# The third hop's result transposed back on 64-row halves of TensorE, with layer 1's other terms in the batches' own order

## The chip, the cores and the metric

The kernel runs on one core of a Trainium2 chip. The metric is the device time of one execution in microseconds, given as the median of several runs. The profile is of one execution, and has its own time.

## The reference, cut to what matters

Two graph layers act on x of 8 batches, 2048 nodes and 64 features. The adjacency `adj` is 2048 x 2048 with random places; in each row all non-zero entries are equal.

```python
# layer 0: weights of its own for each node, from a 16-wide embedding
w = einsum('nd,dkio->nkio', embedding, weight)      # 3 terms k
As = [I, A, 2*(A @ A) - I]
out = einsum('bnki,nkio->bno', einsum('knm,bmc->bnkc', As, x), w) + b
x = layernorm(x + out)
# layer 1: the same two supports, both adj, five terms
x_cat = [x0, A x0, 2 A A x0 - x0, A x0, 2 A A x0 - x0]
out = concat(x_cat) @ weight + bias
x = layernorm(x + out)
```

So there are four products with A ("hops"), two for each layer. For layer 1 the kernel folds the five weights into three, V0, V1 and V2, and computes h V0 + A (h V1 + A (h V2)), where h is layer 0's output. The third hop is A times (h V2), the fourth A times the bracket.

## The kernel before, in words

The 2048 nodes are 16 tiles of 128 rows. A tile of features is 128 nodes by 512 columns (8 batches x 64 features). The values of A are replaced by zeros and ones and a factor for each row (`rcol`), and each feature matrix is split into a high and a low part in a rounded fp32 type, so that two matmuls make up one product.

Stages, in order of time:

1. The first hop (`hop_x`, `add_block`, line 231) and the second hop. The second and the third are done by `seven_products`: A is cut into 2 x 2 quarters, the features too, and seven products of quarters take the place of eight. Line 558 is their matmul. Their result comes out transposed: features on the partitions, nodes along the columns.
2. Layer 0's node-wise mixing (`mix0`, lines 340 to 370): for each tile the operands are transposed (`transpose`, line 274, already on 64-row halves of the array, one half for each of two batches), multiplied with the weights (line 361) and added up on VectorE (line 367). Then comes the layer norm, then `project`.
3. `project` (lines 372 to 390) multiplies a tile of h by the three folded weights (line 380). ScalarE copies the terms h V2 and h V1 to `z[0]` and `z[1]` (line 387), VectorE adds a bias to h V0 and writes it to `z[2]` (line 388). The last tile's `project` runs inside the third hop, after 64 of its matmuls.
4. The third hop (`third`, lines 679 to 683). Its seven products accumulate in two sets of PSUM banks, `sums3[0]` and `sums3[1]`, in turn. `put` (line 577) adds each product to the quarters of the transposed result `zT` in SBUF. When a quarter is finished, `quarter_back` (line 669) queues work in `todo`: `back` (lines 656 to 663) transposes its blocks on TensorE into PSUM banks that are free at that time, and `add_back` (lines 665 to 667) adds them on VectorE, scaled by `rcol`, to `z[1]`. Three of the four quarters go that way, 16 transposes of 128 x 128 each (line 662). The fourth is done inside the fourth hop, at its steps 1 and 3 (lines 791 to 795), 8 transposes each.
5. The fourth hop (`hop_g` and `hop_tile`, lines 767 to 844; line 231), layer 1's norm, and the stores.

`run` (line 242) writes out the order by hand: each step consists of parts with a lead (operands are made up to six steps ahead), and after each step two entries of `todo` are taken. From the last tile of layer 0 to the end of the fourth hop's first part, the order on each engine is kept as written (`in_order`, `ordered`).

The order of batches is what the change turns on. Among four batches of a group g, x has batch number 4g + 2i + j. `mix0` writes it to place 4g + 2j + i (the pattern `(j i)`), and h keeps that mixed order. `project` reads h in halves (its index j is a half of TensorE's rows, i a block of columns) and writes all three terms with the pattern `(i j)`, so they stay in the mixed order up to the output, and the host permutes the output at the end. `back` handles blocks of 128 columns, each with two neighbouring places, whose features lie on the lower and the upper 64 partitions of `zT`.

Of the kernel before, what the change touches and what calls it, by code (L numbers as in the profile page):

```python
# [17 lines left out]
P = 128  # L18
B, N, C = 8, 2048, 64
NT = N // P  # L20
# [17 lines left out]
def pattern(  # L38
# [22 lines left out]
    nc = tc.nc  # L61
# [20 lines left out]
    def bank(name):  # L82

        return psum.tile([P, 2, 512], F32, tag="ps", name=name)
# [7 lines left out]
    z = [z0, [z1[:, t, :] for t in range(NT)], [z2[:, t, :] for t in range(NT)]]  # L92

    def bc(s, t):
        return z[s][t].rearrange("p (b c) -> p b c", c=C)
# [10 lines left out]
    ident = keep.tile([P, P], F32, tag="ident", name="ident")  # L106
# [15 lines left out]
    def ordered(ins):  # L122
        if in_order:
            tc.keep_in_program_order(ins)
# [247 lines left out]
    def project(t, hT, pus=None):  # L372


        for g in range(2):
            pm = bank("pu") if pus is None else pus[g]
            for i in range(2):
                for j in range(2):
                    q = slice(j * C, (j + 1) * C)
                    nc.tensor.matmul(  # L380
                        pm[:, j, i * 3 * C : (i + 1) * 3 * C], lhsT=hT[q, 2 * g + i, :], rhs=v[q],
                        start=True, stop=True,
                    )
            got = pm[:, :, : 6 * C].rearrange("p j (i k c) -> p j i k c", i=2, k=3)
            to = [bc(k, t)[:, 4 * g : 4 * g + 4, :].rearrange("p (i j) c -> p j i c", j=2) for k in range(3)]
            for k in range(2):
                ordered(nc.scalar.copy(to[k], got[:, :, :, 2 - k, :]))
            ordered(nc.vector.tensor_tensor(
                to[2], got[:, :, :, 0, :], bias1.unsqueeze(1).unsqueeze(1).to_broadcast([P, 2, 2, C]), ALU.add,
            ))  # L390
# [4 lines left out]
    BC = B * C // 2  # L395
# [242 lines left out]
    zT, tpool = {}, ExitStack()  # L638
# [6 lines left out]
    def last_projected():  # L645
        project(NT - 1, last_h["T"], (sums3[1][1], sums3[1][0]))
        layer0.close()
        t_pool = pool(tpool, "fzT", 1, reuse_waits="tile")
        for a in range(2):
            for c in range(2):  # L650
                zT[a, c] = t_pool.tile([P, 4, B * C], F32, tag=f"zT{a}{c}", name="zT")
# [3 lines left out]

    def back(ts, pairs, b):

        to = [pairs[n // 4][:, n // 2 % 2, n % 2 * BC : (n % 2 + 1) * BC] for n in range(len(ts))]
        for t, a in zip(ts, to):
            for i in range(2):  # L660
                block = slice((2 * b + i) * P, (2 * b + i + 1) * P)
                nc.tensor.transpose(a[:, i * P : (i + 1) * P], zT[t // 8, t // 4 % 2][:, t % 4, block], ident)  # L662
        return to

    def add_back(t, a, b):
        to = z[1][t][:, b * BC : (b + 1) * BC]
        ordered(nc.vector.scalar_tensor_tensor(to, a, rcol[:, t : t + 1], to, ALU.mult, ALU.add))

    def quarter_back(a, b, which):
        ts, got = range(8 * a, 8 * a + 8), []  # L670

        def two(n):
            for m in (n, n + 1):
                add_back(ts[m], got[m], b)

        work_here = [nothing, nothing, lambda: got.extend(back(ts, sums3[which], b)), nothing]
        return work_here + [lambda n=n: two(n) for n in range(0, 8, 2)]
# [20 lines left out]
    for t in range(NT):  # L698
# [11 lines left out]
        if t == NT - 1:  # L710

            in_order.append(True)
            at = {(1, 0): [between], (1, 1): [lambda: project(t - 1, done["hT"])]}
# [10 lines left out]
        if t > 0:  # L724
            project(t - 1, done["hT"])
# [41 lines left out]
    def hop_g(k):  # L767
# [12 lines left out]
        def use(got):  # L780
            s, hl, end = got["s"], hls[k], k == NT - 1
            if k == 0:
                pairs = [*sums3[1], sums3[0][0]]
                accs[:] = [p[:, i] for p in pairs for i in range(2)]
            add_block(accs[:4], s, hl, k == 0, end)
            waiting.append((s[:, 4 * P :], hl, k == 0, end))
            if k > 0:

                while waiting:
                    add_block(accs[4:], *waiting.pop(0))  # L790
            if k in (1, 3):

                ts = range(8, 12) if k == 1 else range(12, NT)
                for t, a in zip(ts, back(ts, [sums3[0][1]], 0)):
                    add_back(t, a, 0)
            if end:
                for t, a in enumerate(accs):
                    evict(z[2][t], t, a, t % 2)
                bank("skip")
# [53 lines left out]
def general(  # L853
# [10 lines left out]
    nc = tc.nc  # L864
# [11 lines left out]
    z = [zpool.tile([P, 2, B, C], F32, tag=f"z{t}", name=f"z{t}") for t in range(NT)]  # L876


    ident = const.tile([P, P], F32, tag="ident", name="ident")
# [52 lines left out]
    def next_order(o):  # L932

        return o[NT - SLOTS :] + o[: NT - SLOTS]
# [23 lines left out]
    def transpose(src, tag):  # L958

        tt = work.tile([P, B // 2, P], F32, tag=tag, name=tag)  # L960
        pt = ps_tp.tile([P, B // 2, P], F32, tag="tp", name="pt")
        for j in range(B // 2):
            nc.tensor.transpose(pt[:, j, :], src[:, 2 * j : 2 * j + 2, :], ident)
        nc.scalar.copy(tt, pt)
        return tt
# [66 lines left out]
    def project(t, h, u):  # L1032

        hT = transpose(h, "hT")
        for g in range(2):
            pm = ps_mix.tile([P, 2, 512], F32, tag="mix", name="pu")
            for i in range(2):
                for j in range(2):
                    q = slice(j * C, (j + 1) * C)
                    nc.tensor.matmul(  # L1040
                        pm[:, j, i * 3 * C : (i + 1) * 3 * C], lhsT=hT[q, 2 * g + i, :], rhs=v[q],
                        start=True, stop=True,
                    )
            got = pm[:, :, : 6 * C].rearrange("p j (i k c) -> p j i k c", i=2, k=3)
            bs = slice(4 * g, 4 * g + 4)
            for k in range(2):
                nc.scalar.copy(u[t][:, k, bs, :].rearrange("p (i j) c -> p j i c", j=2), got[:, :, :, 2 - k, :])
            nc.vector.tensor_tensor(
                z[t][:, 0, bs, :].rearrange("p (i j) c -> p j i c", j=2), got[:, :, :, 0, :],
                bias1.unsqueeze(1).unsqueeze(1).to_broadcast([P, 2, 2, C]), ALU.add,  # L1050
            )

# [14 lines left out]
    u = [upool.tile([P, 2, B, C], F32, tag=f"u{t}", name=f"u{t}") for t in range(NT)]  # L1067
    order = list(range(NT))
# [6 lines left out]
    order = next_order(order)  # L1075
# [3 lines left out]
    for i, t in enumerate(order):  # L1079
        if behind is not None:  # L1080
            bt, x2 = behind
            tt = [transpose(z[bt][:, 0], "t0"), transpose(z[bt][:, 1], "t1"), transpose(x2, "t2")]
        ph = hop(t, lambda k: z[k][:, 1], ks)
        x2 = work.tile([P, B, C], F32, tag="x2", name="x2")
        nc.vector.scalar_tensor_tensor(x2, ph, 2.0, z[t][:, 0], ALU.mult, ALU.subtract)
        prefetch(order, i, 1)
        if mixed is not None:
            project(*mixed, u)
        if behind is not None:
            mixed = bt, mix0(bt, tt)  # L1090
        behind = (t, x2)
    bt, x2 = behind
    tt = [transpose(z[bt][:, 0], "t0"), transpose(z[bt][:, 1], "t1"), transpose(x2, "t2")]
    project(*mixed, u)
    project(bt, mix0(bt, tt), u)
    ks = order
    order = next_order(order)
# [7 lines left out]
    order = next_order(order)  # L1105
# [66 lines left out]
```

## Time and profile before

| | |
|---|---|
| median of 3 runs | 828.28 us (827.91 to 828.90) |
| the profiled execution's own time | 828.66 us |
| its span, first to last instruction | 826.8 us |
| mean granted TensorE clock | 0.997 |
| TensorE busy | 812.6 us |
| VectorE busy | 594.7 us |
| ScalarE busy | 275.3 us |
| third hop, from its first matmul to the fourth hop's first | 587.0 to 698.7 us |
| fourth hop, to the start of the last chain of norm and store | 698.7 to 809.5 us |
| transposes of `back`, line 662 | 64 of 128 x 128, from 656.8 us on |

A line such as "L662 PE MATMUL accT<-ident,zT" names the line of the kernel, the engine, the operation, and the tiles written and read. PE is TensorE's matmul, PEld its weight load, DVE is VectorE, ACT ScalarE, POOL GpSimd, SP the engine that issues most loads. Matmuls overlap and their ends are modelled, so a group's cost shows in the starts of its matmuls and not in their durations.

### The profile page before, as it was taken

To read this page: it belongs to the slowest core of one execution; us is meant where nothing else is said; L and a number is where in the kernel's file an instruction comes from. 1 tells how busy PE (TensorE), PEld (TensorE's weight loads), DVE (VectorE), ACT (ScalarE), POOL (GpSimd) and SP (SyncE) were. 2 spreads that over 40 slices of the span, in tenths; PEclk is the share of its full clock that TensorE was granted. 3 is DMA by queue.
4 is the path that set the end of the run, shared out by engine and by line. 5 is a ranking of instruction groups with operands and counts; after the bars stand their busy time and mean duration, and the time that the engine had idled before them with its cause. 6 is when DMAs were issued, how large, how long until landed. Compare 5 with 4: busy or idle time off the path is not lost.

```text
span 826.8 us, 14470 instructions
## 1 busy us (share of the span) xinstructions
PE 812.6 (98%) x5614; PEld 725.2 (88%) x5614; DVE 594.7 (72%) x1303; ACT 275.3 (33%) x496; POOL 111.9 (14%) x121
## 2 busy tenths in 40 slices
PE   9999999999999999999999999999999999999995
PEld 6888888888788999999999999999878888888884
DVE  6878658763467888888888888888867546758762
ACT  5436445877401111111111101111287664203110
POOL 0000000000641111111110111111100000003341
PEclk9999999999999999999999999999999999999998
DMA  9997885544200000000000001130154435565631
GB/s 329 376 386 244 287 315 174 155 143 148 69 3 12 15 13 15 14 14 14 14 14 14 30 13 38 39 103 27 43 150 152 141 128 150 167 181 165 212 120 42
DMA packets 70940, 96.54 MB, mean 117 GB/s; under 512 B 4432, under 2 KB 45648, under 8 KB 70736
## 3 DMA queue, kind: packets, MB, share of 16 engines
q1 hardware_dynamic: 61616, 78.49, 29.5%
q10 hardware_dynamic: 6944, 8.66, 3.0%
q0 software_dynamic: 2304, 8.39, 2.8%
q8 instruction: 46, 0.75, 0.4%
q14 instruction: 30, 0.25, 0.1%
HBM read 78.75 MB, written 16.78 MB: 116 GB/s over the span
## 4 chain that ended last, share of the span: by engine, by line
PE 92%; issue 3%; DVE 3%; POOL 1%; ACT 1%; DVEq 0%; POOLq 0%; ACTq 0%
PE pm L361 36%; PE accT L558 24%; PE acc L231 14%; PE a L231 8%; PE accT L231 5%; PE pu L380 2%; DVE acc L367 2%; POOL z L609 1%; PE pt L274 1%; PE accT L662 1%; PE first L135 1%; POOL xc L322 0%; POOL got L337 0%; ACT sq L310 0%; DVE s L200 0%
## 5 line engine op out<-in xcount | busy, mean ns | idle before, releaser
L367 DVE SCALAR_TENSOR_TENSOR acc<-pm,pack_sb,acc 128x256 f32<-128x256 f32 x512 | 246.3, 483 | 41.6 <-PE pm L361 20.5
L558 PE MATMUL accT<-s,hl 128*128 128x512 f32 x896 | 205.6, 390 | 1.9 <-DVE s L200 1.4
L558 PEld LDWEIGHTS accT<-s,hl 128*128 128x128 f32 x896 | 167.6, 188 | 37.7 <-issue 1.8
L361 PE MATMUL pm<-w,xt 64*128 64x256 f32 x1024 | 160.9, 378 | 1.1 <-DVE acc L367 1.1
L361 PE MATMUL pm<-w,t 64*128 64x256 f32 x1024 | 160.0, 376 | 0.2 <-ACT t L276 0.2
L361 PE MATMUL pm<-w,z 64*128 64x256 f32 x1024 | 159.9, 376 | 0.0
L231 PE MATMUL acc<-hl,s 128*128 128x512 f32 x512 | 117.1, 390 | 0.0
L546 ACT CAST s<-raw 128x1024 fp32r<-128x1024 bf16 x96 | 101.0, 1052 | 40.2 <-ACT hl L211 32.2
L231 PEld LDWEIGHTS acc<-hl,s 128*128 128x128 f32 x512 | 95.8, 188 | 21.1 <-DVE hl L215 0.7
L361 PEld LDWEIGHTS pm<-w,t 64*128 64x128 f32 x1024 | 110.7, 187 | 1.9 <-ACT t L276 0.6
L361 PEld LDWEIGHTS pm<-w,z 64*128 64x128 f32 x1024 | 110.8, 187 | 1.4
L361 PEld LDWEIGHTS pm<-w,xt 64*128 64x128 f32 x1024 | 108.4, 187 | 2.5 <-issue 1.2
L276 ACT COPY hT<-pt 128x512 f32<-128x512 f32 x15 | 8.8, 587 | 197.4 <-PE pt L274 197.4
L231 PE MATMUL a<-hl,s 128*128 128x512 f32 x320 | 73.0, 389 | 0.0
L231 PEld LDWEIGHTS a<-hl,s 128*128 128x128 f32 x320 | 60.0, 188 | 12.5
L211 ACT CAST hl<-z 128x256 fp32r<-128x256 f32 (+1 forms) x96 | 47.1, 510 | 67.6 <-PE acc L231 36.4
L215 DVE TENSOR_TENSOR hl<-z,hl 128x512 fp32r<-128x512 f32 (+1 forms) x96 | 52.5, 552 | 21.2 <-ACT hl L211 18.4
L322 POOL TENSOR_TENSOR xc<-acc,s 128x512 f32<-128x512 f32 x16 | 16.7, 1043 | 279.5 <-DVE s L320 265.4
L200 DVE TENSOR_SCALAR s<-raw 128x1024 fp32r<-128x1024 f32 x47 | 33.2, 706 | 16.5 <-PE acc L231 10.9
L231 PE MATMUL accT<-hl,s 128*128 128x512 f32 x192 | 44.2, 390 | 0.0
L231 PEld LDWEIGHTS accT<-hl,s 128*128 128x128 f32 x192 | 35.9, 188 | 7.4
L347 POOL TENSOR_TENSOR acc<-z,ebias 128x256 f32<-128x256 f32 x32 | 22.7, 731 | 90.5 <-DVE hl L215 87.2
(105 smaller groups left out, 603.3 us busy)
## 6 DMA issues: line engine op xcount, KB each, us to landing
raw<-in_adj SPq DMA_DIRECT2D x67, 512.0 KB, 4.7
raw<-sums_of SPq DMA_DIRECT2D x64, 256.0 KB, 2.8
sums_of<-z POOLq DMA_DIRECT2D x16, 512.0 KB, 6.3
raw<-quarters SPq DMA_DIRECT2D x32, 256.0 KB, 2.6
raw<-in_adj SPq DMA_DIRECT2D x16, 384.0 KB, 3.5
quarters<-seen ACTq DMA_DIRECT2D x16, 256.0 KB, 6.2
xt<-in_xT SPq DMA_DIRECT2D x16, 256.0 KB, 2.6
out<-got ACTq DMA_DIRECT2D x16, 256.0 KB, 3.9
```

The source lines that it names most:

```text
L200: ordered(nc.vector.tensor_scalar(s, raw, 0.0, None, ALU.not_equal))
L211: ordered(nc.scalar.copy(to[0], src))
L215: ordered(nc.vector.tensor_tensor(to[1], src, to[0], ALU.subtract))
L231: nc.tensor.matmul(accs[i], lhsT=s[:, i * P : (i + 1) * P], rhs=hl[h], start=(first and h == 0), stop=(last and h == 1),)
L276: ordered(nc.scalar.copy(tt.rearrange("p j (h n) -> p h j n", h=2), pt[:, :, : B // 2 * C].rearrange("p h (j n) -> p h j n", n=C)))
L322: ordered(nc.gpsimd.tensor_tensor(xc, src, wide(s), ALU.subtract))
L347: nc.gpsimd.tensor_tensor(part.rearrange("p (j i) c -> p j i c", j=2), bc(0, t)[:, 4 * g : 4 * g + 4, :].rearrange("p (i j) c -> p j i c", ...
L361: nc.tensor.matmul(pm[:, j, i], lhsT=tt[k][q, 2 * g + i, :], rhs=w[k][q, ds, :], start=(k == 0), stop=(k == 2),)
L367: ordered(nc.vector.scalar_tensor_tensor(part, pm[:, :, :, d, :].rearrange("p j i c -> p (j i) c"), emb_sb[:, t, dd : dd + 1], part, ALU.m ...
L380: nc.tensor.matmul(pm[:, j, i * 3 * C : (i + 1) * 3 * C], lhsT=hT[q, 2 * g + i, :], rhs=v[q], start=True, stop=True,)
L546: ordered(nc.scalar.copy(s, got["raw"]))
L558: nc.tensor.matmul(acc[i][:, c], lhsT=hl[h][:, i * P : (i + 1) * P], rhs=S[:, c * 512 : (c + 1) * 512], start=(kk == 0 and h == 0), stop=( ...
```

## The change

`back` no longer transposes a 128 x 128 block in one instruction. It takes the lower and the upper 64 partitions of `zT` apart, with one transpose for each on its half of the array's rows (index j), 64 columns wide; each half's results go to a PSUM bank of its own. So there are 128 transposes in place of 64. A tile's result then lies in two banks, 128 columns in each, and its halves are ordered `(j i)`: the batches' own order. `add_back` reads this two-bank layout and adds it to `z[1]`. For the terms to fit together, `project` writes `z[1]` and `z[2]` in the pattern `(j i)` as well; `z[0]`, the operand of the third hop, stays in `(i j)`. The output is then in the batches' own order, and the host's permutation becomes a plain one. The fallback `general`, which runs only if a flag is set, gets the same change of order in its own `project`.

```diff
@@ project
-            to = [bc(k, t)[:, 4 * g : 4 * g + 4, :].rearrange("p (i j) c -> p j i c", j=2) for k in range(3)]
+            order = ["p (i j) c -> p j i c", "p (j i) c -> p j i c", "p (j i) c -> p j i c"]
+            to = [bc(k, t)[:, 4 * g : 4 * g + 4, :].rearrange(order[k], j=2) for k in range(3)]
@@ back
-        to = [pairs[n // 4][:, n // 2 % 2, n % 2 * BC : (n % 2 + 1) * BC] for n in range(len(ts))]
+        to = [pairs[n // 4][:, :, n % 4 * P : (n % 4 + 1) * P] for n in range(len(ts))]
         for t, a in zip(ts, to):
             for i in range(2):
                 block = slice((2 * b + i) * P, (2 * b + i + 1) * P)
-                nc.tensor.transpose(a[:, i * P : (i + 1) * P], zT[t // 8, t // 4 % 2][:, t % 4, block], ident)
+                for j in range(2):
+                    q = slice(j * C, (j + 1) * C)
+                    nc.tensor.transpose(
+                        a[:, j, i * C : (i + 1) * C], zT[t // 8, t // 4 % 2][q, t % 4, block], ident[q, q]
+                    )
@@ add_back
-        to = z[1][t][:, b * BC : (b + 1) * BC]
+        to = z[1][t][:, b * BC : (b + 1) * BC].rearrange("p (j n) -> p j n", j=2)
@@ kernel, on the host
-    got = got.reshape(NT, P, 2, 2, 2, C).transpose(2, 4, 3, 0, 1, 5)
-    return lay(got.reshape(B, N, C))
+    return lay(got.transpose(2, 0, 1, 3).reshape(B, N, C))
```

More of the change, by code (lines that the diff above doesn't have):

```diff
@@ L1046, in project @@
             for k in range(2):
-                nc.scalar.copy(u[t][:, k, bs, :].rearrange("p (i j) c -> p j i c", j=2), got[:, :, :, 2 - k, :])
+                nc.scalar.copy(u[t][:, k, bs, :].rearrange("p (j i) c -> p j i c", j=2), got[:, :, :, 2 - k, :])
             nc.vector.tensor_tensor(
-                z[t][:, 0, bs, :].rearrange("p (i j) c -> p j i c", j=2), got[:, :, :, 0, :],
+                z[t][:, 0, bs, :].rearrange("p (j i) c -> p j i c", j=2), got[:, :, :, 0, :],
                 bias1.unsqueeze(1).unsqueeze(1).to_broadcast([P, 2, 2, C]), ALU.add,
```

## The prediction

> **What bounds the kernel now.** I read the page first (busy shares, then the chain that ended last), then the chain in order of time around the change, then the rows of the transposes themselves, and last the starts of single matmuls.
>
> ```profile
> PE 812.6 (98%) x5614; PEld 725.2 (88%) x5614; DVE 594.7 (72%) x1303; ACT 275.3 (33%) x496; POOL 111.9 (14%) x121
> ...
> PE 92%; issue 3%; DVE 3%; POOL 1%; ACT 1%; DVEq 0%; POOLq 0%; ACTq 0%
> ```
>
> TensorE is busy for 98% of the span and makes 92% of the chain. So a change is worth what it takes from TensorE's own row of work, unless it is made in one of the few places where TensorE waits. The chain in order of time shows whether the third hop has such places:
>
> ```profile
> 606.15 51.09 PE accT L558 x224
> 657.24 1.75 PE accT L662 x16
> 658.99 14.55 PE accT L558 x64
> ...
> 704.31 0.87 PE accT L662 x8
> ...
> 744.21 65.29 PE a L231 x288
> ```
>
> From 606.15 us to 809.50 us the chain is TensorE without a break. The 64 transposes that the change rewrites (line 662: three groups of 16 and two of 8) stand in it with their whole length. TensorE's idle time before any of them is zero. Here time saved on TensorE is time saved at the end, one for one, as long as no other engine comes late.
>
> What one transpose costs cannot be read from its duration, because matmuls overlap. The first row below is the form of before, the second a form with the shape of the new one, from layer 0's `transpose` at line 274 (64 rows of the array, 64 columns out):
>
> ```profile
> L662 PE MATMUL accT<-ident,zT x64: 270/273/273, 657.1 to 711.2; 128*128 128x128 f32 x64
> ```
>
> ```profile
> L274 PE MATMUL pt<-ident,xc x120: 216/222/224, 265.5 to 575.1; 64*128 64x64 f32 x120
> ...
> L274 PE MATMUL accT<-ident,xc x8: 222/223/271, 599.8 to 600.0; 64*128 64x64 f32 x8
> ```
>
> 273 against 222 ns says little. What counts is from one start to the next, so I took the starts from the timeline of TensorE (start, length, count). Three places matter: a group of 16 of before, a group of 8 of before, and the only place where eight transposes on half arrays stand between full-array matmuls of the third hop, which is just what the change makes everywhere:
>
> ```profile
> 656.62 0.62 PE L558 MATMUL accT<-s,hl 128*128 128x512 f32 x2
> 657.08 1.91 PE L662 MATMUL accT<-ident,zT 128*128 128x128 f32 x16
> 658.74 1.17 PE L558 MATMUL accT<-s,hl 128*128 128x512 f32 x4
> ```
>
> ```profile
> 704.15 1.03 PE L662 MATMUL accT<-ident,zT 128*128 128x128 f32 x8
> 704.94 1.17 PE L231 MATMUL accT<-hl,s 128*128 128x512 f32 x4
> ```
>
> ```profile
> 599.45 0.40 PE L558 MATMUL accT<-s,hl 128*128 128x512 f32 x1
> 599.78 0.46 PE L274 MATMUL accT<-ident,xc 64*128 64x64 f32 x8
> 600.17 0.96 PE L558 MATMUL accT<-s,hl 128*128 128x512 f32 x3
> ```
>
> The last row set is for the pace of a long run of the new form (two groups of 8, back to back, in layer 0):
>
> ```profile
> 424.72 0.44 PE L274 MATMUL pt<-ident,xc 64*128 64x64 f32 x8
> 424.97 0.44 PE L274 MATMUL pt<-ident,z 64*128 64x64 f32 x8
> 425.21 0.68 PE L361 MATMUL pm<-w,xt 64*128 64x256 f32 x4
> ```
>
> **What the Trainium skill says.** "TensorEngine Tiling (Array Packing)", Key Properties: changing the tiling mode drains TensorE, and different tiles can load and multiply in parallel. The trace agrees with both. From the last full-array matmul to the first half-array transpose is 327 ns (599.454 to 599.781), where it is 233 ns to a full-array one (656.844 to 657.077); on the way out it is 153 ns against 29. And the two halves of a pair start 3 to 4 ns apart. "TensorE: Matmul & The Clock Gate", Back-to-back issue gap: up to 64 columns a matmul does not go below about 25 ns. The trace shows 31 (16 in 0.49 us), so the page leaves at most 12 ns a pair. The tiling page's Gotcha 1, PSUM Pressure, says that different row tiles cannot be in one PSUM bank at the same time. The change gives each half its own bank (index j), as line 274 does; no run here shows a clash. "VectorE: DVE Perf Modes", Why PSUM operands drop a tier: an fp32 operation with a PSUM operand runs at the plain rate however it is laid out. So I expect no faster mode from the new write order of `project`; its row at line 388 is 415 ns now.
>
> **The change, part by part.**
>
> *Transposes (`back`).* Removed are 64 transposes 128x128, added 128 of 64 rows by 128 columns, in alternating halves. I count what a group adds to TensorE's row: from the last matmul before it to the third after it, less three normal intervals. A normal interval is 0.2274 us (224 matmuls from 606.15 to 657.08), three are 0.682. The third matmul after it is needed because the first ones behind a group also come late (312 ns instead of 227).
> - 16 of before: 656.844 to 659.285 is 2.441, less 0.682 = 1.759 us.
> - 8 of before: 703.917 to 705.486 is 1.569, less 0.682 = 0.886 us.
> - 8 of the new form: 599.454 to 600.745 is 1.291, less 0.682 = 0.609 us, both mode switches in it.
> - Each further pair of the new form: 62.5 ns (62 in the long run of layer 0, 63 inside the group at 599.78).
> - So 16 of the new form cost 0.609 + 4 x 0.0625 = 0.859, and 32 cost 0.609 + 12 x 0.0625 = 1.359 us.
> - Saved: 3 x (1.759 - 1.359) = 1.20, and 2 x (0.886 - 0.859) = 0.05. Together 1.25 us.
>
> The unit cost that before does not show is the pair's pace over 32 in a row. From below it is bounded by 50 ns (twice the page's 25), which would save 44 further pairs x 12.5 = 0.55 more, 1.80 in all. From above I put 75 ns, about halfway to the 91 at which the 44 further pairs would eat up the 1.25; that gives back 0.55 and leaves 0.70. I take 62.5, since it is measured with the same shapes and types.
>
> *Adding back (`add_back`).* The 32 operations at line 667 (476 ns) now read two banks instead of one. Line 367 reads across two banks in the same kind of instruction and takes 483: 32 x 7 ns, and on VectorE. VectorE is not late: the next group that writes the same bank pair comes at 698.70, when the add-backs of the group before ended at 693.96, and the 4 at 705.22 end at 706.88, before the transposes at 710.48. What VectorE makes behind those 4 adds (step 4 of the fourth hop) is ready at 708.35 and used at 711.28. So cover of 2.9 to 4.7 us lies over this; if it were gone, the cost would be 0.2 us. A t's result now lies in both banks of its pair, so bank 0 is free after four add-backs and not after two: 0.8 us later, inside the same 4.7.
>
> *Write order in `project`.* Of three results per call two change the order of their writes; same number of instructions, elements and engines, and the order of all instructions on every queue stays as it was. 30 of the 32 calls lie in layer 0, where TensorE waited 1.1 us for VectorE in total: nothing to gain or lose there. The last two lie in the third hop and do stop TensorE (0.56 us at 606.15, behind two ScalarE copies of 0.66 and one VectorE add of 0.43). Contiguous writes might take some ns off, or add some: I put 0, with 0.05 us either way.
>
> *The host's final permutation* and the fallback `general` cost nothing here: the one is outside of the device, the other is branched over.
>
> **Sum.** The profiled execution took 828.66 us (span 826.8 and 1.86 around it): less 1.25 is 827.4. It lies 0.38 above the median of the three runs, 828.28, so against the median I forecast 827.0, 0.15% faster. About 0.2% (1.66 us) is what a measurement of this kernel can tell from no change, so the likeliest case is "within".
>
> **Rivals.**
> 1. *Forecast:* pace of 62.5 ns, one for one: 827.0. Chance 0.66.
> 2. *The run of 32 goes at the floor:* longer than any run of before, it may settle nearer to half of a full transpose (109 / 2 = 54) or the page's 50 ns: 1.6 to 1.8 saved, 826.5. For it: the first pair inside a full-array stretch is slow (110 ns) and spoils the short groups. Against it: in layer 0 the pace of 62 does not fall over 8 pairs. Chance 0.20.
> 3. *Another engine takes the time back:* the operands of the fourth hop would come late. VectorE is busy 7.2 of the 9 us from 690 to 699 and 22.0 of the 33 from 711, ScalarE less, and TensorE waits nowhere: the cover of 2.9 us is more than the 1.25. It would give 828.3. Chance 0.09.
> 4. *Slower: the halves take turns.* If the two half-array transposes of a pair do not overlap in the third hop, because both read one zT tile while VectorE and ScalarE work on SBUF, each of the 64 pairs costs 62.5 ns more, 4.0 us, and the sum turns to +2.75: 831.0. It decides from a pair of 82 ns on (62.5 + 1.25 us / 64). Against it: the pairs at 599.78 overlap in that very stage. Chance 0.05.
>
> **Numbers.** The three runs lie within 827.91 to 828.90, so I add 0.5 us on both sides: the forecast with its bounds (0.70 to 1.80 saved) is 826.5 to 827.6. The low end is rival 2 less this scatter, 826.0; the high end reaches to rival 3, 828.3; rival 4 and some scatter are left out, about 1.5 in 10. Faster by over 0.2% means under 826.6: two thirds of rival 2 and a tenth or more of the forecast by scatter, 0.24. Slower by over 0.2%: rival 4, 0.05. Within: 0.71.
>
> **What would show it.** Right: in `back`'s new row 128 transposes with starts 3 to 36 ns apart, pairs 62; a group of 32 that adds 1.36 us and one of 16 that adds 0.86; entry 327 and exit 153 ns; rows of `add_back` near 480 ns; TensorE without new idle time after 606. Wrong: pairs near 54 (rival 2) or near 125 (rival 4); idle time of TensorE released by VectorE or ScalarE (rival 3); a different length of layer 0, before 606 us, where I expect none.

## The result, and the profile after

Over 22 runs each, the changed kernel takes 827.14 us (826.67 to 827.75) and the kernel before 828.39 us (827.91 to 828.90). The ratio is 0.9986, with a 95% interval of 0.9980 to 0.9991: 1.25 us or 0.15% faster, well beyond chance, though under the 0.2% that the prediction took for the least a measurement can tell: 22 runs of each kernel tell a smaller one.

On the page, TensorE's row is shorter by 1.8 us of busy time (812.6 before), although 64 matmuls were added (5678 instead of 5614). That is more than the change made, as the table of stretches below shows. The rows of the other engines stand within 0.1 us of before.

```profile
PE 810.8 (98%) x5678; PEld 722.8 (88%) x5678; DVE 594.8 (72%) x1303; ACT 275.3 (33%) x496; POOL 111.9 (14%) x121
```

The chain in order of time shows the same unbroken run of TensorE as before, with shorter pieces where the transposes stand (start, length, what):

```profile
605.95 51.09 PE accT L560 x224
657.04 1.15 PE accT L667 x32
658.19 14.73 PE accT L560 x64
...
702.89 0.65 PE accT L667 x16
...
742.73 65.29 PE a L231 x288
```

The pieces of the transposes went from 1.75 to 1.15 us, but do not take these differences as the gain. The piece of matmuls behind each of the three large groups grew (14.55 to 14.73 us after the first): most of that is the exit from the half-array mode (153 ns against 29 before, see the starts below), which the chain books on the next line. This is why the prediction counted from a matmul before the group to the third one after it. The timeline of TensorE gives those starts:

```profile
656.43 0.61 PE L560 MATMUL accT<-s,hl 128*128 128x512 f32 x2
656.98 1.22 PE L667 MATMUL accT<-ident,zT 64*128 64x64 f32 x32
658.12 1.20 PE L560 MATMUL accT<-s,hl 128*128 128x512 f32 x4
```

```profile
702.28 0.61 PE L231 MATMUL accT<-hl,s 128*128 128x512 f32 x2
702.82 0.72 PE L667 MATMUL accT<-ident,zT 64*128 64x64 f32 x16
703.47 1.20 PE L231 MATMUL accT<-hl,s 128*128 128x512 f32 x4
```

From the first half-array start to the next full-array start is 1.15 us for 32 and 0.64 for 16 (before: 1.67 for 16 and 0.79 for 8). The single starts say the rest: 319 ns from the last full-array matmul to the first transpose (before: 233), 152 to 154 ns on the way out (before: 28 to 29), the first pair 111 to 112 ns, each further pair 60 to 65.

Cut at landmarks of TensorE, the two profiled executions differ so:

| stretch on TensorE | before | after | difference |
|---|---|---|---|
| start to line 558/560 behind the last `project` | 606.15 | 605.95 | -0.20 |
| from there to the first matmul of `hop_tile` (all five groups lie here) | 137.89 | 136.61 | -1.28 |
| from there to the flag's matmul (line 748/755) | 69.00 | 69.00 | 0.00 |
| from there to the end of the span | 13.71 | 13.30 | -0.41 |

The second row is the change. The first and the last hold none of the rewritten transposes, and their differences lie within the scatter: over the nine traces on record they run from 605.95 to 607.06 us and from 13.30 to 13.71, whichever form of transposes a kernel has. The medians move by 1.25 and not by the 1.9 us of the two spans.

### The profile page after: what moved, and what is told of

Same layout as the page of the kernel before. It is cut to its first block, busy times and chain, and to the rows that moved or that the text cites. A ratio compares the mean times of both kernels' runs of the same rounds, so it can differ in the third digit from the quotient of the medians.

```text
span 824.9 us, 14598 instructions
## 1 busy us (share of the span) xinstructions
PE 810.8 (98%) x5678; PEld 722.8 (88%) x5678; DVE 594.8 (72%) x1303; ACT 275.3 (33%) x496; POOL 111.9 (14%) x121
## 4 chain that ended last, share of the span: by engine, by line
PE 91%; issue 3%; DVE 3%; POOL 1%; ACT 1%; DMA 1%; DVEq 0%; POOLq 0%; ACTq 0%
PE pm L361 36%; PE accT L560 24%; PE acc L231 14%; PE a L231 8%; PE accT L231 5%; PE pu L380 2%; DVE acc L367 2%; POOL z L611 1%; PE pt L274 1%; PE accT L667 1%; DMA z<-in_x 1%; POOL xc L322 0%; POOL got L337 0%; ACT sq L310 0%; DVE s L200 0%
```

## The experiments

Under test is the prediction's sum, in other terms: 0.609 us for eight transposes on halves is a fixed 0.36 us for entering and leaving the mode and 62.5 ns for each 128 x 128 block. The main rivals: the write order carries a part of the gain; the gain comes from narrower outputs and not from two halves at work at once; the switches are free; another engine takes time back.

### The transposes alone

From the changed kernel:

```diff
-            order = ["p (i j) c -> p j i c", "p (j i) c -> p j i c", "p (j i) c -> p j i c"]
+            order = ["p (i j) c -> p j i c"] * 3
```

> The transposes and the add-backs are as in the changed kernel, and project writes all three terms in the old order. (The transposed result is then added to terms whose batches lie in another order, so the values are not the reference's; the work is the same.) The sum of the prediction puts the whole gain on the transposes: 1.25 us below before, about 827.1, as the changed kernel. The rival that the new write order carries a part of the gain expects less than 0.9 us. Groups on TensorE: 32 transposes add 1.36 us, 16 add 0.86.

Measured: 827.11 us (826.41 to 827.62), a ratio to before of 0.9985 (0.9979 to 0.9992). The groups add the same as in the changed kernel, within 1 ns on the same starts, and the stretch of TensorE that holds all five (the second row of the table) takes 136.59 us, in the changed kernel 136.61. The transposes alone give the whole gain.

### The write order alone

From the kernel before: the old transposes, and `project` with the new `order` list of the diff.

> The transposes and the add-backs are as before, and project writes two of its terms in the new order. (Again the values are not the reference's.) The sum expects the time of before within 0.1 us, project's rows at 375 and 415 ns, and TensorE's stop of 0.56 us behind the last project unchanged. The rival expects a part of the 1.25 us here.

Measured: 828.16 us (828.00 to 828.75), ratio 1.0000 (0.9992 to 1.0009). VectorE's rows of `project` in this kernel:

```profile
L389 DVE TENSOR_TENSOR z<-pu,pack_sb x30: 413/415/425, 273.3 to 581.1; 128x256 f32<-128x256 f32 x30
L389 DVE TENSOR_TENSOR z<-accT,pack_sb x2: 424/424/424, 605.9 to 606.5; 128x256 f32<-128x256 f32 x2
```

Medians of 415 and 424 ns (the middle one of the three numbers), as before. TensorE's stop behind the last `project` is 0.55 us, before 0.56, and the stretch with the five groups takes 137.88 us, before 137.89. Writing contiguous columns instead of strided ones is worth nothing here.

### One half after the other

From the changed kernel, the loop over halves moved outside of the loops over tiles and blocks (the transpose itself, not shown, is the same):

```diff
-        for t, a in zip(ts, to):
-            for i in range(2):
-                block = slice((2 * b + i) * P, (2 * b + i + 1) * P)
-                for j in range(2):
-                    q = slice(j * C, (j + 1) * C)
+        for j in range(2):
+            q = slice(j * C, (j + 1) * C)
+            for t, a in zip(ts, to):
+                for i in range(2):
+                    block = slice((2 * b + i) * P, (2 * b + i + 1) * P)
```

> The changed kernel, but each group transposes all lower halves first and then all upper ones, so that no two neighbours lie on different halves. If the gain comes from two halves at work at once, it goes: one half-array transpose then takes what a pair takes or more, 62 ns or up to the 109 ns of a full one, so 64 pairs cost 64 x 62 = 4.0 us more than the changed kernel or up to 64 x (218 - 62) = 10 us more. If the gain comes from 64 columns out in place of 128 alone, the time stays at 827.1.

Measured: 830.10 us (829.61 to 830.44), ratio 1.0022 (1.0012 to 1.0032): slower than before. The same 32 transposes now take 1.95 us from their start to the next full-array matmul, where they took 1.15:

```profile
657.50 2.03 PE L667 MATMUL accT<-ident,zT 64*128 64x64 f32 x32
659.45 2.79 PE L560 MATMUL accT<-s,hl 128*128 128x512 f32 x11
```

Away from the crossing from the lower to the upper half, and after the first, their starts lie 60 to 65 ns apart. So one half-array transpose takes as long as a pair does, and in a pair the second one is free. The gain needs this overlap: two transposes one after the other take about 125 ns, more than the 109 of a full one. It needs the shorter half-array transpose as well (62 against 109 ns), so 64 columns out in place of 128 are not the whole cause, but they are a part of it. What sets the 62 ns was not tested. With the halves the kernel also alternates PSUM banks, but a change of bank alone brings no overlap: in this kernel the eighth and the ninth transpose of a group of 32 lie on the same half and go to different banks, and they start 63 to 65 ns apart.

The kernel lost 3.0 us against the changed one and not the 4.0 expected: by the starts, 0.81 for each group of 32 and 0.30 for each of 16. The difference is at the crossing, where the trace of each group shows three starts 6 to 10 ns behind the one before: three overlaps that the expectation left out. At about 62 ns each, in five groups, they make 0.93 of the missing 1.0 us.

### Twice the transposes, in either form

```diff
-        for t, a in zip(ts, to):
+        for t, a in 2 * list(zip(ts, to)):
```

made in the changed kernel's `back`, and in the one of before.

> The changed kernel with every group's transposes done twice over (the second writes the same values again), so groups of 64 and 32. The sum expects 64 more pairs at 62.5 ns, 4.0 us above the changed kernel, with the mode switches paid once as there. If long runs settled at the pace of the issue limit (50 to 54 ns), it would be 3.2 to 3.4 us; if the switches were part of the pace, more than 5.

> The kernel before with every group's full transposes done twice. The sum has 109 ns for one full transpose and nothing for leaving and entering: 64 more make 7.0 us above before. Together with the kernel of halves done twice it gives the price of a 128 x 128 block in either form without any mode switch: 109 against 62 ns.

Measured: 831.58 us (831.12 to 832.04), ratio 1.0041 (1.0027 to 1.0054), for halves, and 835.36 us (835.26 to 835.62), ratio 1.0087 (1.0073 to 1.0100), for full transposes. The second is 6.98 us above its own before, as expected. The first is 4.4 us above the changed kernel's median where 4.0 was expected; its five runs leave about 1 us on either side, and the starts in the trace are sharper. Halves:

```profile
658.06 2.23 PE L667 MATMUL accT<-ident,zT 64*128 64x64 f32 x64
660.22 1.20 PE L560 MATMUL accT<-s,hl 128*128 128x512 f32 x4
```

Full:

```profile
657.17 3.66 PE L662 MATMUL accT<-ident,zT 128*128 128x128 f32 x32
660.59 1.40 PE L558 MATMUL accT<-s,hl 128*128 128x512 f32 x5
```

From start to next line 2.16 us for 64 halves against 1.15 for 32: 16 more pairs in 1.01 us, 63 ns each, with no sign of the faster pace that rival 2 has for long runs. Full: 3.42 against 1.67, 16 more in 1.75 us, 109 ns each. Over the five groups the starts give 4.05 and 6.99 us more.

### Three groups split in two

From the changed kernel's `quarter_back`:

```diff
-        work_here = [nothing, nothing, lambda: got.extend(back(ts, sums3[which], b)), nothing]
+        def four(n):
+            got.extend(back(ts[4 * n : 4 * n + 4], sums3[which][n : n + 1], b))
+
+        work_here = [nothing, nothing, lambda: four(0), nothing, lambda: four(1)]
```

> The changed kernel with each of its three groups of 32 half-array transposes split in two of 16, one step of the third hop apart. The number of transposes is the same, the mode switches are three pairs more. If an entry and an exit cost 0.36 us, as the prediction took from the one group before, it is 3 x 0.36 = 1.08 us slower than the changed kernel, about 828.2, and the gain is all but gone. If the switches cost nothing and the group's fixed part is something else, the time stays at 827.1.

Measured: 828.21 us (827.45 to 828.97), ratio 0.9997 (0.9988 to 1.0005). The number of transposes is that of the changed kernel, and its gain is gone. The timeline shows both parts of the first group, one step of eight matmuls apart:

```profile
657.81 0.71 PE L667 MATMUL accT<-ident,zT 64*128 64x64 f32 x16
658.46 2.11 PE L560 MATMUL accT<-s,hl 128*128 128x512 f32 x8
660.49 0.71 PE L667 MATMUL accT<-ident,zT 64*128 64x64 f32 x16
661.14 1.19 PE L560 MATMUL accT<-s,hl 128*128 128x512 f32 x4
```

For one group, 0.64 us twice against 1.15 once makes 0.14 of the 0.36 us lost; the rest is outside of the transposes, in 320 ns ahead of each group instead of 227 and in the slow start of the matmuls behind it. Three more entries and exits cost 1.07 us by the medians, 0.36 each; by the starts, counted to the third matmul behind each group, it is 0.34.

### The last two groups made one

From the changed kernel, in `hop_g`:

```diff
-            if k > 0:
+            if k > 1:
                 while waiting:
                     add_block(accs[4:], *waiting.pop(0))
-            if k in (1, 3):
-                ts = range(8, 12) if k == 1 else range(12, NT)
-                for t, a in zip(ts, back(ts, [sums3[0][1]], 0)):
+            if k == 1:
+                ts = range(8, NT)
+                for t, a in zip(ts, back(ts, sums3[0], 0)):
                     add_back(t, a, 0)
```

> The changed kernel with the fourth quarter's two groups of 16 half-array transposes made one of 32 at the fourth hop's step 1, in both bank pairs of sums3[0]; the two last row blocks' sums begin one step later. It saves one entry and one exit: 0.36 us below the changed kernel, about 826.8, if nothing comes late. The rival: eight add-backs in a row (3.2 us of VectorE) at step 1 delay the operands of step 4 beyond their cover of 2.9 us, or the matmuls at step 2 wait for the banks; then TensorE shows idle time there, and the time is at or above the changed kernel's.

Measured: 826.72 us (826.20 to 827.02), ratio to before 0.9980 (0.9973 to 0.9988). This is 0.42 below the changed kernel's median; the intervals of the two ratios overlap, so the medians alone do not prove it. The trace does show the place: two groups of 16 added 0.85 each, the one of 32 adds 1.35, 0.35 us less.

```profile
701.28 1.22 PE L667 MATMUL accT<-ident,zT 64*128 64x64 f32 x32
702.43 9.83 PE L231 MATMUL accT<-hl,s 128*128 128x512 f32 x42
```

TensorE has no idle time behind it, though VectorE now does eight add-backs in a row ahead of the operands for step 4:

```profile
702.21 3.22 DVE L674 SCALAR_TENSOR_TENSOR z<-accT,rcol,z 128x256 f32<-128x256 f32 x8
705.50 0.96 DVE L207 SCALAR_TENSOR_TENSOR s<-raw,rrow 128x768 fp32r<-128x768 f32 x1
```

Those operands are begun at 705.50, 7.94 us after the hop's first matmul at 697.56. In the changed kernel it was 7.87 us (705.16 and 697.29), behind four add-backs that could start only later, at 703.58. So the eight hardly touched the cover, and it wasn't put to the test. This kernel is the fastest of all that were run.

## Why the prediction was right

*Transposes.* The sum gave 1.359 and 0.859 us for the new groups. Counted in the prediction's own way, they add 1.352 to 1.361 and 0.846 to 0.853, the old ones 1.759 to 1.761 and 0.887. That is 1.28 us saved in all, against 1.25 forecast: 1.21 in the three large groups and 0.07 in the two small ones. The entry took 319 ns where 327 was expected. The fixed part, which came from a single group of eight behind a single stretch, held in all five groups and in the split (0.34 to 0.36 each). That the medians differ by just the 1.25 us of the forecast is in part luck: their interval reaches from 0.75 to 1.66 us.

*Pace over long runs.* It was the cost that before does not show. 62.5 ns was taken out of a range of 50 to 75; it is 63 over 16 further pairs and shows no drift. The long run of layer 0 that gave it was not quite the new form: there the starts lie 36 to 37 and 19 to 28 ns apart in turn, in the new groups 3 to 4 and 56 to 62, which the prediction's sign (3 to 36 ns) does not describe. The pace of a pair is the same in both. Rival 2, the issue limit, falls: by the Trainium skill's "TensorE: Matmul & The Clock Gate", Back-to-back issue gap, 25 ns would be the least for one matmul, but here a half-array transpose is not bound by issue. The two of a pair start 3 to 4 ns apart, so that figure does not hold from one half to the other; and a transpose takes 60 to 65 ns on its half even with nothing beside it, as the kernel with one half after the other shows.

*The slower case.* The halves do not take turns. The kernel with one half after the other shows most of what that would have cost: the order of the loops is the difference between 1.25 us faster and 1.9 us slower than before.

*Add-backs.* Reading two banks costs nothing: the median (the middle one of the three numbers) is 476 ns, as before, where 7 ns more were allowed. The first line is before, the second after:

```profile
L667 DVE SCALAR_TENSOR_TENSOR z<-accT,rcol,z x32: 473/476/485, 658.2 to 712.7; 128x256 f32<-128x256 f32 x32
L674 DVE SCALAR_TENSOR_TENSOR z<-accT,rcol,z x32: 473/476/484, 657.7 to 711.1; 128x256 f32<-128x256 f32 x32
```

TensorE has no idle time from its first matmul behind the last `project` (605.95 us) to the flag's matmul, in this kernel as in the one before; rival 3 did not come about. How wide the cover on VectorE is was not tested.

*Write order.* Nothing, as put, and the kernel with the order alone agrees, by its medians within 0.7 us, and on TensorE, by the stop behind the last `project` and the stretch of the groups, within 0.02.

*From TensorE to the end.* One for one: 1.28 us in the stretch of the groups, the same 69.00 us behind it, and 1.25 us between the medians.

## What to carry to other kernels

A transpose on two halves of the array was worth it here where the halves alternate and the group is long. With the numbers of this case (0.36 us for a mode switch and back, 46 ns saved for each 128 x 128 block) it pays from about eight blocks on. Merging two groups into one saved 0.35 us, about ten times what the change itself saved in a group of eight blocks. Cost a group from a matmul before it to a few behind it, since a part of a mode switch shows on the neighbours' lines. Where TensorE was the chain without a break, such a count of starts agreed with the medians, each kernel's against the runs of before that belong to it, within 0.2 us in all kernels but one: with halves done twice it gave 2.8 us where the medians, over five runs, gave 3.4.

## What the runs showed of the hardware that had not been expected

At the crossing from lower to upper halves, in the kernel that does one half first, three pairs overlap and not one. In order of program the upper half's first transpose comes after the lower half's last; only one pair could then start together if every start waited its turn. In the first group the starts read 64, 7, 55, 58, 7, 55, 7, 54, 63 ns apart. One reading is that some transposes of the upper half started ahead of earlier ones of the lower half. The records do not tell which half a transpose belongs to, and two on the same half that started close together would look alike. So the cause stays open; only the starts are shown.
